# A layer of gated experts on one core: ScalarE in written order in the first unit, result blocks turned back over two units, early operands stored a step later

## The chip, the core and the metric

The kernel runs on one core of one Trainium2 chip. The metric is device microseconds of one execution. Engines are named as in the profile: PE is TensorE, ACT ScalarE, DVE VectorE, POOL GpSimd, and SP is the engine that issues most DMAs.

## What is computed

x has 8 batch rows of 512 x 256 numbers, in float32. Each of 8 experts, and one shared expert, is a gated pair of products and a product back; the results are weighted per batch row and added to x:

```python
g = jnp.einsum('bsd,edf->ebsf', h, Wg)
u = jnp.einsum('bsd,edf->ebsf', h, Wu)
expert_outs = jnp.einsum('ebsf,efd->ebsd', jax.nn.silu(g) * u, Wd)
expert_output = jnp.einsum('be,ebsd->bsd', gating_probs, expert_outs)
shared = jnp.einsum('bsf,fd->bsd', jax.nn.silu(h @ Sg) * (h @ Su), Sd)
sg = shared_gate_prob[:, :, None]
return x + (1.0 - sg) * expert_output + sg * shared
```

D is 256, F is 1024, and no expert is skipped.

## The kernel before

**Units.** The work is cut into 36 units: two halves of the batch (four rows each, `NI` = 4), nine experts, two groups of 512 columns of F. A unit's name is half_expert_group, as in `1_0_1`; `u.n` counts them.

**gate_up (L499).** For each unit the gate and up products of four rows with four blocks of columns are made from fewer matmuls than the plain way needs. Four plain steps give the products of a row with the block of its own number: `P_step` (L335, weight times x) and `Q_step` (L367, into the same bank, with a prepared weight `at` and the other half of x). ScalarE copies P out (L342), DVE makes Q (L375). The twelve products of unlike numbers come in six pairs (`PAIRS`, L59). A pair needs one matmul with differences (`R1_step`, L378: weight difference `u`, operand difference `v`) and two with sums (`R_step`, L389: `wb` and `b`), seeded with sums `z` of P and Q (L354 on POOL, L356 on DVE). `finish` (L320) applies silu on ScalarE (L323) and, on DVE, the product with the up part and the coefficient (L329).

The weights are prepared beside this: `load_w` (L247) issues two loads of 128 KB on SP, `make_at` (L270) makes `at`, `w_difference` (L284) and `w_sums` (L290) make `u` and `wb` on POOL, with prescales on ScalarE (L267). The operands `v` and `b` are made once in each half, in its first unit or ahead of it, are stored in DRAM (`xs`), and are loaded again by each later unit (L190, L207).

**down (L414).** The products back, for the unit before, are 14 groups of two matmuls, so 28 steps, in seven-product form (sums `T` on POOL, L411). Each group takes one of two banks, `po0` and `po1`, in turn (`new_po`, L120). If the bank has not just been used for a transpose (`turned`), ScalarE seeds it with the accumulator (L429) and copies it out at the end (L453); otherwise DVE adds the accumulator (L449). A written string `ORDER` (L561) interleaves the steps of `gate_up` (G) with those of `down` (D); the first unit has `FIRST`.

**Change of half.** In the last unit of the first half, `turn_x` (L141) transposes the four x rows of the second half on PE, and `make_forms` (L164) makes and stores the first three pairs' operands ahead. When the last `down` of that half has completed a block of the result, it is put on the list `ends`. `turn_back` (L478) transposes such a block on PE into the bank last used, ScalarE copies it to `to` (L490; one buffer), POOL adds it to the loaded part of x, `xr` (L491), and SP stores the sum (L494) and loads the next `xr` (two buffers, shared with `xin`). There are eight blocks. A block is taken from the list ahead of a D step (L612), whenever there is one.

**Who sets the order.** PE and POOL run in the written order (`manual_schedule`, L566). ScalarE, DVE and SP are ordered by the scheduler of the language, which may move an instruction ahead of others that it does not depend on. Each DMA has one of eight semaphores in turn, and waits until the DMA before it on the same semaphore has landed. `make_coef` (L96) loads the gates on ScalarE's queue, makes `rest` (L106) and `coef` (L108, L109) on DVE.

Of the kernel before, what the change touches and what calls it, by code (L numbers as in the profile page):

```python
# [9 lines left out]
F32 = mybir.dt.float32  # L10
# [6 lines left out]
def kernel(  # L17
# [31 lines left out]
    nc = tc.nc  # L49
    B, S, D = x.shape  # L50
    E, _, F = Wg.shape
    P = 128
# [6 lines left out]
    PAIRS = ((1, 0), (0, 2), (3, 0), (1, 2), (3, 1), (3, 2))  # L59
    ZBANK = 2  # L60
    LATE = (4, 5)

    const = ctx.enter_context(tc.tile_pool(name="const", bufs=1))
    wpool = ctx.enter_context(tc.tile_pool(name="w", bufs=5))
# [45 lines left out]

    scratch = {}
    back = {}
    xhub = {}


# [48 lines left out]
    def make_forms(h, p):  # L164

        i, j = PAIRS[p]
        d = CI[i] - CI[j]
        v, b0, b1 = (
            zpool.tile([P, S], F32, tag="z", name=f"f{k}{h}_{p}") for k in range(3)
        )  # L170
        ve.tensor_sub(v, xhub[h, i][:, 0], xhub[h, j][:, 0])
        if d != 1.0:
            nc.scalar.mul(v, v, 1.0 / d)
        ve.tensor_add(b0, v, xhub[h, j][:, 1])
        gp.tensor_tensor(b1, v, xhub[h, i][:, 1], ALU.add)
        scratch[h, p] = dram.tile([P, 3, S], F32, tag=f"xs{h}_{p}", name=f"xs{h}_{p}")
        for k, t in enumerate((v, b0, b1)):
            nc.sync.dma_start(scratch[h, p][:, k], t)

    def x_difference(u, p):  # L180

        i, j = PAIRS[p]
        v = vpool.tile([P, S], F32, tag="v", name=f"v{u.name}_{p}")
        if (u.h, p) not in scratch:
            d = CI[i] - CI[j]
            ve.tensor_sub(v, xhub[u.h, i][:, 0], xhub[u.h, j][:, 0])  # L186
            if d != 1.0:
                nc.scalar.mul(v, v, 1.0 / d)
        else:
            nc.sync.dma_start(v, scratch[u.h, p][:, 0])  # L190
        u.V[p] = v

    def x_sums(u, p):


        i, j = PAIRS[p]
        v = u.V[p]
# [72 lines left out]
    def make_at(u, i):  # L270
# [10 lines left out]
        scaled_sum(t, CI[i], raw[:, :, 0], raw[:, :, 1], False)  # L281
        u.at[i] = t

    def w_difference(u, p):  # L284
        i, j = PAIRS[p]
        U = upool.tile([P, 2, P], F32, tag="u", name=f"u{u.name}_{p}")
        gp.tensor_tensor(U, u.at[i], u.at[j], ALU.subtract)  # L287
        u.U[p] = U

    def w_sums(u, p):  # L290
        i, j = PAIRS[p]
        d = CI[i] - CI[j]
        W = bpool.tile([P, 2, 2, P], F32, tag="wb", name=f"wb{u.name}_{p}")
# [41 lines left out]
    def P_step(u, i, m):  # L335
        bank = new_bank(u, m, f"c{i}{i}")
        u.bank[i, i, m] = bank
        nc.tensor.matmul(  # L338
            bank, u.raw[i][:, m, 0], xhub[u.h, i][:, 0], start=True, stop=True
        )  # L340
        t = ppool.tile([P, S], F32, tag="p", name=f"P{i}{m}_{u.name}")
        nc.scalar.copy(t, bank)  # L342
        u.Ps[i, m] = t
        for p in range(ZBANK):
            a, b = PAIRS[p]
            if max(a, b) == i:
                new_z(u, p, m, i, bank if u.n or p else None)

    def new_z(u, p, m, i, bank=None):
# [7 lines left out]
        u.z[i, o, m] = z  # L357

    def make_z(u, p, m):
        if p in LATE:  # L360
            return
        for i in PAIRS[p]:
            o = sum(PAIRS[p]) - i
            if (i, o, m) not in u.z:
                new_z(u, p, m, i)

    def Q_step(u, i, m):  # L367
# [7 lines left out]
        ve.tensor_sub(t, bank, u.Ps[i, m])  # L375
        u.Qs[i, m] = t

    def R1_step(u, p, m):  # L378
        i, j = PAIRS[p]
        bank = new_bank(u, m, f"c{j}{i}")  # L380
# [4 lines left out]
        first = u.Ps if p in LATE else u.z  # L385
        ve.tensor_sub(seed, first[(i, m) if p in LATE else (i, j, m)], bank)  # L386
        ve.tensor_add(bank, bank, first[(j, m) if p in LATE else (j, i, m)])  # L387

    def R_step(u, p, m, r):  # L389
        i, j = PAIRS[p] if r == 0 else PAIRS[p][::-1]  # L390
        bank = u.bank[i, j, m]
        nc.tensor.matmul(  # L392
            bank, u.W[p][:, r, m], u.VB[p][:, r],
            start=False, stop=True, skip_group_check=True,
        )
        if p in LATE:
            ve.tensor_add(bank, bank, u.Qs[j, m])  # L397
        finish(u, m, i, j, bank)

# [99 lines left out]
    def gate_up(u, nxt):  # L499
# [6 lines left out]
            x_sums(u, p)  # L506
            w_sums(u, p)

        for p, make in ((0, w_difference), (0, w_sums), (1, w_difference), (1, w_sums), (2, w_difference)):
            make(u, p)  # L510
        ahead = ((0, x_difference), (0, x_sums), (1, x_difference), (1, x_sums), (2, x_difference))
        if u.n:
            for p, make in ahead:
# [19 lines left out]
        for p in range(len(PAIRS)):  # L533
# [29 lines left out]


    ends = []
    with tc.manual_schedule(engines={mybir.EngineType.PE, mybir.EngineType.Pool}):  # L566
        touch_banks()
        loaded = []
        for i in range(NI):
            loaded.append(load_rows(tpool, "t", i))  # L570
            load_w(units[0], i)
        turning = turn_x(0, tpool, "t", loaded)
        for _ in range(2):
            next(turning)
        for m in range(2):
            P_step(units[0], 0, m)
        for i in range(NI):
            make_at(units[0], i)
        make_coef()
        behind, acc = iter(()), {}  # L580
        for u in units:
            final = u.closes
            nxt = units[u.n + 1] if u.n + 1 < len(units) else None
            g = gate_up(u, nxt)
            nG = 0
            for what in ORDER if u.n else FIRST:
                if what == "G":
                    if nG == 4 and u.n:
                        for _ in behind:
                            pass  # L590
                        pv = units[u.n - 1]
                        load_d(pv, (1,))
                        if pv.opens:
                            acc = {}
                        behind = down(pv, acc, pv.closes)
                        if pv.closes:
                            load_back(pv.h, *BACK[0])
                    if final and nxt is not None:
                        if nG == 18:
                            turning = turn_x(u.h + 1, iopool, "io")  # L600
                        if nG >= 18 and nG % 3 == 0:
                            next(turning, None)
                        if nG in (42, 45, 48):
                            make_forms(u.h + 1, nG // 3 - 14)
                    next(g)
                    nG += 1
                    if nxt is None and nG in (18, 24, 30, 36, 42):
                        next(behind, None)
                elif u.n == 0:
                    for _ in range(2):  # L610
                        next(turning, None)
                else:  # L612
                    if ends:
                        turn_back(*ends.pop(0))
                    next(behind, None)
            for _ in g:
                pass
            for _ in turning:
                pass
        for _ in behind:  # L620
            pass
        pv = units[-1]
        load_d(pv, (1,))
        step, due = 0, []
        for n, at in enumerate(BACK):
            load_back(NH - 1, *at, *((zpool, "z") if n < 6 else (iopool, "io")))
        for _ in down(pv, acc, True):
            step += 1
            if due and due[0] < step:
                due.pop(0)  # L630
                turn_back(*ends.pop(0))
            due += [step + 1] * (len(ends) - len(due))
        for end in ends:
            turn_back(*end)
# [1 line left out]
_INS = [  # L636
    "x",
# [33 lines left out]
```

## Time and profile before

| | |
|---|---|
| median of three runs | 2524.63 us (2524.19 to 2526.6) |
| the profiled execution | 2525.02 us |
| its span, first to last instruction | 2523.2 us |
| mean granted clock of TensorE | 0.998 |
| PE busy | 2499.9 us (99%) |
| POOL busy | 1927.0 us (76%) |
| DVE busy | 1495.5 us (59%) |
| ACT busy | 1143.4 us (45%) |
| matmuls of `gate_up` with sums, L392 | 1728, 594 ns each |
| z on POOL, L354 | 434, 1273 ns each |
| bytes moved | 242.94 MB, 96 GB/s |

A row of the profile's timeline has the start and the length of a run of like instructions, the engine, the line, the operation with its tiles and shape, the number of instructions, and in brackets the time for which the engine was idle before, with what ended it. A busy PE is not one at its peak: the matmuls overlap, so that 594 ns is the length of one, while a row of four starts 1.72 us after the row before it. "PEq", "ACTq" and "SPq" are the sequencers of those engines; a DMA issue stands under them.

### The profile page before, as it was taken

How to read it: one execution, taken by the hardware profiler on the slowest of the kernel's cores; microseconds unless marked ns; L12 is line 12 of the kernel's file. 1: busy time of each engine (PE TensorE's matmuls, PEld its weight loads, DVE VectorE, ACT ScalarE, POOL GpSimd, SP SyncE). 2: the span in 40 equal slices, each digit the busy share in tenths (PEclk: the TensorE clock that was granted, in tenths of full speed). 3: DMA queues.
4: the chain of work that ended last, by engine and by line, in shares of the span. 5: the costliest groups of instructions: out<-in, count | busy, mean ns of one | idle time of the engine just before them, and what ended most of it. 6: DMA issues, size and time to landing. Idle time of an engine off the chain costs nothing.

```text
span 2523.2 us, 22099 instructions
## 1 busy us (share of the span) xinstructions
PE 2499.9 (99%) x5896; PEld 1108.5 (44%) x5896; DVE 1495.5 (59%) x2257; ACT 1143.4 (45%) x2079; POOL 1927.0 (76%) x2073
## 2 busy tenths in 40 slices
PE   8999999999999999999999999999999999999999
PEld 3444444444444444444444444444444444444444
DVE  7655565565555555555775555555565555555556
ACT  3344444444444444444323444444444444444443
POOL 7878877777787777877788777877777777777874
PEclk9999999999999999999999999999999999999999
DMA  5222233233333332233443322232233332332222
GB/s 183 89 86 90 86 94 92 84 101 96 100 92 92 95 90 82 88 96 96 142 140 111 92 89 87 88 95 89 84 101 96 100 93 91 98 89 80 89 84 83
DMA packets 181036, 242.94 MB, mean 96 GB/s; under 512 B 13872, under 2 KB 122416, under 8 KB 180912
## 3 DMA queue, kind: packets, MB, share of 16 engines
q1 hardware_dynamic: 180624, 241.49, 31.5%
q8 instruction: 49, 0.80, 0.1%
q14 instruction: 75, 0.61, 0.1%
q10 hardware_dynamic: 288, 0.04, 0.0%
HBM read 227.84 MB, written 13.63 MB: 96 GB/s over the span
## 4 chain that ended last, share of the span: by engine, by line
PE 95%; POOL 2%; DVE 1%; issue 1%; DMA 0%; ACT 0%; ACTq 0%; SPq 0%; POOLq 0%; DVEq 0%
PE po L438 33%; PE c L392 28%; PE c L382 14%; PE c L338 10%; PE c L369 10%; POOL z L354 1%; POOL T L411 1%; DMA w<-in_L_cond_Wu_dram 0%; POOL wb L268 0%; DMA sgt<-ondB_sharedgateprob_dram 0%; PE pto L129 0%; POOL b L201 0%; POOL u L287 0%; PE ptx L129 0%; DVE v L186 0%
## 5 line engine op out<-in xcount | busy, mean ns | idle before, releaser
L392 PE MATMUL c<-b,wb 128*128 128x512 f32 x1728 | 817.4, 594 | 3.4 <-POOL wb L268 3.4
L354 POOL TENSOR_TENSOR z<-P,Q 128x512 f32<-128x512 f32 x434 | 542.4, 1273 | 110.1 <-DVE Q L375 66.9
L329 DVE SCALAR_TENSOR_TENSOR h<-sg,coef,c 128x512 f32<-128x512 f32 x576 | 427.1, 742 | 239.5 <-PE c L392 230.1
L453 ACT COPY acc<-po 128x512 f32<-128x512 f32 x476 | 278.8, 586 | 584.9 <-PE po L438 582.0
L392 PEld LDWEIGHTS c<-b,wb 128*128 128x128 f32 x1728 | 328.6, 191 | 415.5 <-issue 391.2
L323 ACT ACTIVATE sg<-c 128x512 f32<-128x512 f32 x576 | 342.5, 596 | 367.1 <-PE c L392 202.8
L411 POOL TENSOR_TENSOR T<-h,h 128x512 f32<-128x512 f32 x284 | 358.3, 1277 | 112.1 <-PE po L438 70.4
L438 PE MATMUL po<-T,sd 128*128 128x512 f32 x864 | 435.3, 593 | 2.6 <-ACT po L429 2.6
L382 PE MATMUL c<-v,u 128*128 128x512 f32 x864 | 436.3, 593 | 0.7 <-DVE Q L375 0.7
L386 DVE TENSOR_TENSOR c<-z,c 128x512 f32<-128x512 f32 x288 | 200.1, 695 | 328.0 <-ACT sg L323 256.1
L411 POOL TENSOR_TENSOR T<-h,T 128x512 f32<-128x512 f32 x284 | 356.5, 1276 | 6.7 <-PE po L438 6.7
L268 POOL TENSOR_TENSOR wb<-wb,u 128x256 f32<-128x256 f32 x216 | 154.5, 735 | 206.7 <-ACT wb L267 206.7
L397 DVE TENSOR_TENSOR c<-c,Q 128x512 f32<-128x512 f32 x288 | 200.2, 697 | 188.0 <-PE c L392 188.0
L438 PE MATMUL po<-h,wd 128*128 128x512 f32 x576 | 294.6, 594 | 4.4 <-ACT to L490 4.4
L429 ACT COPY po<-acc 128x512 f32<-128x512 f32 x464 | 273.7, 590 | 36.2 <-DVE acc L455 14.3
L338 PE MATMUL c<-x,w 128*128 128x512 f32 x576 | 276.5, 593 | 2.8 <-ACT sg L323 1.4
L375 DVE TENSOR_TENSOR Q<-c,P 128x512 f32<-128x512 f32 x288 | 198.0, 688 | 106.9 <-ACT sg L323 106.6
L382 PEld LDWEIGHTS c<-v,u 128*128 128x128 f32 x864 | 164.4, 190 | 208.3 <-issue 189.4
L438 PEld LDWEIGHTS po<-T,sd 128*128 128x128 f32 x864 | 163.7, 190 | 208.5 <-issue 188.5
L342 ACT COPY P<-c 128x512 f32<-128x512 f32 x288 | 168.3, 585 | 129.9 <-PE c L338 129.9
L369 PE MATMUL c<-x,at 128*128 128x512 f32 x432 | 203.1, 592 | 1.5 <-DVE z L356 1.5
L387 DVE TENSOR_TENSOR c<-c,z 128x512 f32<-128x512 f32 x288 | 199.5, 693 | 0.9 <-POOL z L354 0.9
(68 smaller groups left out, 1870.8 us busy)
## 6 DMA issues: line engine op xcount, KB each, us to landing
b<-xs SPq DMA_DIRECT2D x207, 512.0 KB, 3.5
v<-xs SPq DMA_DIRECT2D x207, 256.0 KB, 2.6
w<-in_L_cond_Wg_dram SPq DMA_DIRECT2D x128, 128.0 KB, 3.4
w<-in_L_cond_Wu_dram SPq DMA_DIRECT2D x128, 128.0 KB, 3.3
wd<-in_L_cond_Wd_dram SPq DMA_DIRECT2D x64, 256.0 KB, 2.7
xs<-b SPq DMA_DIRECT2D x9, 512.0 KB, 3.1
xin<-in_x_dram SPq DMA_DIRECT2D x16, 256.0 KB, 4.1
xr<-in_x_dram SPq DMA_DIRECT2D x16, 256.0 KB, 3.2
```

Source lines behind the costliest of these rows:

```text
L323: nc.scalar.activation(s, bank, AF.Silu)
L329: ve.scalar_tensor_tensor(t, u.sg[i, j], coef[:, u.e, b : b + 1], bank, ALU.mult, ALU.mult)
L338: nc.tensor.matmul(bank, u.raw[i][:, m, 0], xhub[u.h, i][:, 0], start=True, stop=True)
L354: gp.tensor_tensor(z, u.Ps[i, m], u.Qs[o, m], ALU.add)
L369: nc.tensor.matmul(bank, u.at[i][:, m], xhub[u.h, i][:, 1], start=False, stop=True, skip_group_check=True,)
L382: nc.tensor.matmul(bank, u.U[p][:, m], u.V[p], start=True, stop=True)
L392: nc.tensor.matmul(bank, u.W[p][:, r, m], u.VB[p][:, r], start=False, stop=True, skip_group_check=True,)
L397: ve.tensor_add(bank, bank, u.Qs[j, m])
L411: eng.tensor_tensor(t, a, b, ALU.subtract)
L429: nc.scalar.copy(po, acc[J, x])
L438: nc.tensor.matmul(po, u.wd[I][x], b, start=first, stop=True, skip_group_check=not first,)
L453: nc.scalar.copy(acc[J, x], po)
```

## The change

1. **The first unit.** ScalarE joins PE and POOL in the written order until the first unit's steps are written, and then leaves it: the block of `manual_schedule` is closed and another opened with PE and POOL alone.
2. **The fourth `at`.** `make_at(nxt, 3)`, which was the last one made ahead, is made by the next unit itself, before its third difference.
3. **Stores of the early operands.** `make_forms` no longer stores; it puts the tiles on a list, and `store_made` stores them three G steps later, or before the last pair.
4. **Turnings.** A block of the result is turned only when `since_close`, the number of D steps since the last `down` of the half began, has reached the next of 7, 12, 17, ... 42. Before, a block was turned at the first D step after its completion.
5. **Plain products.** A way of making a pair of the first unit with plain matmuls comes in (`plain`, `plain_step`), and constants `LATE0` and `PLAIN` for it; `PLAIN` is empty and `LATE0` equals `LATE`.

```diff
+    LATE0 = (4, 5)
+    PLAIN = ()
...
         gp.tensor_tensor(b1, v, xhub[h, i][:, 1], ALU.add)
-        scratch[h, p] = dram.tile([P, 3, S], F32, tag=f"xs{h}_{p}", name=f"xs{h}_{p}")
-        for k, t in enumerate((v, b0, b1)):
-            nc.sync.dma_start(scratch[h, p][:, k], t)
+        made.append((h, p, (v, b0, b1)))
+
+    def store_made():
+        for h, p, tiles in made:
+            scratch[h, p] = dram.tile([P, 3, S], F32, tag=f"xs{h}_{p}", name=f"xs{h}_{p}")
+            for k, t in enumerate(tiles):
+                nc.sync.dma_start(scratch[h, p][:, k], t)
+        made.clear()
...
-        for p, make in ((0, w_difference), (0, w_sums), (1, w_difference), (1, w_sums), (2, w_difference)):
+        for p, make in ((0, w_difference), (0, w_sums), (1, w_difference), (1, w_sums)):
             make(u, p)
+        if u.n:
+            make_at(u, 3)
+        w_difference(u, 2)
...
                 if p >= 2:
                     load_w(nxt, p - 2)
-                    make_at(nxt, p - 2)
+                    if p < 5:
+                        make_at(nxt, p - 2)
             store_forms(u)
+            if u.n == 0 and p == 4:
+                for q in PLAIN:
+                    make_forms(0, q)
+            if p == 5:
+                store_made()
...
-    with tc.manual_schedule(engines={mybir.EngineType.PE, mybir.EngineType.Pool}):
+    since_close = 0
+    BACK_AT = [7 + 5 * k for k in range(8)]
+    HAND = {mybir.EngineType.PE, mybir.EngineType.Pool}
+    by_hand = ExitStack()
+    by_hand.enter_context(
+        tc.manual_schedule(engines=HAND | {mybir.EngineType.Activation})
+    )
...
                     if pv.closes:
                         load_back(pv.h, *BACK[0])
+                        since_close = 0
...
                     if nG in (42, 45, 48):
                         make_forms(u.h + 1, nG // 3 - 14)
+                    if nG in (45, 48, 51):
+                        store_made()
...
             else:
-                if ends:
+                since_close += 1
+                if ends and since_close >= BACK_AT[0]:
+                    BACK_AT.pop(0)
                     turn_back(*ends.pop(0))
                 next(behind, None)
         for _ in g:
             pass
+        if u.n == 0:
+            by_hand.close()
+            by_hand.enter_context(tc.manual_schedule(engines=HAND))
```

More of the change, by code (lines that the diff above doesn't have):

```diff
@@ L112 @@
     back = {}
+    made = []
     xhub = {}
@@ L175, in make_forms @@
         gp.tensor_tensor(b1, v, xhub[h, i][:, 1], ALU.add)
[L176 to L178 removed]
+        made.append((h, p, (v, b0, b1)))
[5 more added lines that the diff above has]
+        made.clear()
     def x_difference(u, p):
         i, j = PAIRS[p]
+        if plain(u, p):
+            return
         v = vpool.tile([P, S], F32, tag="v", name=f"v{u.name}_{p}")
@@ L196, in x_sums @@
         i, j = PAIRS[p]
+        if plain(u, p):
+            return
         v = u.V[p]
@@ L282, in make_at, with late, plain @@
         u.at[i] = t
+    def late(u):
+        return LATE if u.n else LATE0
+    def plain(u, p):
+        return u.n == 0 and p in PLAIN
     def w_difference(u, p):
         i, j = PAIRS[p]
+        if plain(u, p):
+            return
         U = upool.tile([P, 2, P], F32, tag="u", name=f"u{u.name}_{p}")
@@ L292, in w_sums @@
         d = CI[i] - CI[j]
+        if plain(u, p):
+            u.W[p] = []
+            for r, (k, c) in enumerate(((i, CI[j]), (j, CI[i]))):
+                a, A = u.raw[k][:, :, 0], u.raw[k][:, :, 1]
+                if c != 0.0:
+                    t = upool.tile([P, 2, P], F32, tag="u", name=f"m{u.name}_{p}_{r}")
+                    scaled_sum(t, c, a, A, False)
+                    A = t
+                u.W[p].append(A)
+            return
         W = bpool.tile([P, 2, 2, P], F32, tag="wb", name=f"wb{u.name}_{p}")
@@ L345, in P_step @@
             a, b = PAIRS[p]
-            if max(a, b) == i:
+            if max(a, b) == i and not plain(u, p):
                 new_z(u, p, m, i, bank if u.n or p else None)
@@ L359, in make_z @@
     def make_z(u, p, m):
-        if p in LATE:
+        if p in late(u) or plain(u, p):
             return
@@ L376, in Q_step, with plain_step @@
         u.Qs[i, m] = t
+    def plain_step(u, p, m, r, k):
+        i, j = PAIRS[p] if r == 0 else PAIRS[p][::-1]
+        if k == 0:
+            u.bank[i, j, m] = new_bank(u, m, f"c{i}{j}")
+        nc.tensor.matmul(
+            u.bank[i, j, m], u.W[p][r][:, m] if k else u.raw[i][:, m, 0],
+            xhub[u.h, j][:, k], start=k == 0, stop=k == 1,
+        )
+        if k:
+            finish(u, m, i, j, u.bank[i, j, m])
     def R1_step(u, p, m):
         i, j = PAIRS[p]
+        if plain(u, p):
+            for k in range(2):
+                plain_step(u, p, m, 0, k)
+            return
         bank = new_bank(u, m, f"c{j}{i}")
@@ L384, in R1_step @@
         u.bank[i, j, m] = seed
-        first = u.Ps if p in LATE else u.z
-        ve.tensor_sub(seed, first[(i, m) if p in LATE else (i, j, m)], bank)
-        ve.tensor_add(bank, bank, first[(j, m) if p in LATE else (j, i, m)])
+        first = u.Ps if p in late(u) else u.z
+        ve.tensor_sub(seed, first[(i, m) if p in late(u) else (i, j, m)], bank)
+        ve.tensor_add(bank, bank, first[(j, m) if p in late(u) else (j, i, m)])
     def R_step(u, p, m, r):
+        if plain(u, p):
+            plain_step(u, p, m, 1, r)
+            return
         i, j = PAIRS[p] if r == 0 else PAIRS[p][::-1]
@@ L395, in R_step @@
         )
-        if p in LATE:
+        if p in late(u):
             ve.tensor_add(bank, bank, u.Qs[j, m])
@@ L565 @@
     ends = []
-    with tc.manual_schedule(engines={mybir.EngineType.PE, mybir.EngineType.Pool}):
[L567 to L610, printed above, removed]
-                        next(turning, None)
-                else:
-                    if ends:
-                        turn_back(*ends.pop(0))
-                    next(behind, None)
[L616 to L620, printed above, removed]
-            pass
[L622 to L634, printed above, removed]
@@ new lines @@
+    since_close = 0
[4 more added lines that the diff above has]
+        tc.manual_schedule(engines=HAND | {mybir.EngineType.Activation})
+    )
+    touch_banks()
+    loaded = []
+    for i in range(NI):
+        loaded.append(load_rows(tpool, "t", i))
+        load_w(units[0], i)
+    turning = turn_x(0, tpool, "t", loaded)
+    for _ in range(2):
+        next(turning)
+    for m in range(2):
+        P_step(units[0], 0, m)
@@ new lines @@
+    for i in range(NI):
+        make_at(units[0], i)
+    make_coef()
+    behind, acc = iter(()), {}
+    for u in units:
+        final = u.closes
+        nxt = units[u.n + 1] if u.n + 1 < len(units) else None
+        g = gate_up(u, nxt)
+        nG = 0
+        for what in ORDER if u.n else FIRST:
+            if what == "G":
+                if nG == 4 and u.n:
+                    for _ in behind:
+                        pass
+                    pv = units[u.n - 1]
+                    load_d(pv, (1,))
+                    if pv.opens:
+                        acc = {}
+                    behind = down(pv, acc, pv.closes)
+                    if pv.closes:
+                        load_back(pv.h, *BACK[0])
+                        since_close = 0
+                if final and nxt is not None:
+                    if nG == 18:
+                        turning = turn_x(u.h + 1, iopool, "io")
+                    if nG >= 18 and nG % 3 == 0:
+                        next(turning, None)
+                    if nG in (42, 45, 48):
+                        make_forms(u.h + 1, nG // 3 - 14)
+                    if nG in (45, 48, 51):
+                        store_made()
+                next(g)
+                nG += 1
+                if nxt is None and nG in (18, 24, 30, 36, 42):
+                    next(behind, None)
+            elif u.n == 0:
+                for _ in range(2):
+                    next(turning, None)
+            else:
+                since_close += 1
+                if ends and since_close >= BACK_AT[0]:
+                    BACK_AT.pop(0)
+                    turn_back(*ends.pop(0))
+                next(behind, None)
+        for _ in g:
+            pass
+        if u.n == 0:
+            by_hand.close()
+            by_hand.enter_context(tc.manual_schedule(engines=HAND))
+        for _ in turning:
+            pass
@@ L636 @@
+    for _ in behind:
+        pass
+    pv = units[-1]
+    load_d(pv, (1,))
+    step, due = 0, []
+    for n, at in enumerate(BACK):
+        load_back(NH - 1, *at, *((zpool, "z") if n < 6 else (iopool, "io")))
+    for _ in down(pv, acc, True):
+        step += 1
+        if due and due[0] < step:
+            due.pop(0)
+            turn_back(*ends.pop(0))
+        due += [step + 1] * (len(ends) - len(due))
+    for end in ends:
+        turn_back(*end)
+    by_hand.close()
 _INS = [
```

## The prediction

> **What bounds the kernel now.** I read the chain of work that ended last first, then TensorE's waits, then the timelines of the stretches where those waits lie.
>
> The chain, section 4 of the page:
>
> ```profile
> PE 95%; POOL 2%; DVE 1%; issue 1%; DMA 0%; ACT 0%; ACTq 0%; SPq 0%; POOLq 0%; DVEq 0%
> ```
>
> TensorE is the bound: only its stalls can be won, and a delay elsewhere costs only where TensorE then waits. Its waits by line (total us, times, longest), those over 0.4 us:
>
> ```profile
> PE po L438 <- ACT to L490: 4.4, 2, 3.6
> PE c L392 <- POOL wb L268: 3.4, 1, 3.4
> PE po L438 <- ACT po L429: 2.6, 2, 2.2
> PE c L369 <- DVE z L356: 1.5, 1, 1.5
> PE c L338 <- ACT sg L323: 1.4, 1, 1.4
> ...
> PE c L338 <- DVE h L329: 0.5, 1, 0.5
> ```
>
> Nearly every wait happens once or twice in 36 units, so the middle is gap-free (rows of four matmuls repeat every 1.72 us). I added up each matmul's start-to-start excess over 0.429 us (0.109 for a transpose): 29.1 us in all, 13.6 in the first unit (before 70 us), about 13 around the change of half (1192 to 1340), 1.8 at the end. So 26.6 us are within reach. Three parts of the change reach there.
>
> Part of the excess is a slowed clock after a stall. The stretches right behind three stalls (columns: time, busy and count of PE, PEld, DVE, ACT, POOL, then granted clock, DMA share, GB/s):
>
> ```profile
> 50.30:53.60 3.30, 3.30 (x5) 1.24 (x5) 1.30 (x2) 1.05 (x2) 3.30 (x5) 0.50 0.26 86
> ...
> 1238.10:1241.50 3.40, 3.40 (x5) 1.35 (x4) 1.77 (x3) 1.58 (x4) 3.32 (x6) 0.50 0.96 323
> ...
> 1289.30:1292.70 3.40, 3.32 (x4) 1.52 (x5) 0.00 (x0) 0.03 (x1) 3.39 (x4) 0.50 0.64 234
> ```
>
> Clock 0.50 for 3.41 us, so about 1.7 us lost each, on top of the stall.
>
> [...]
>
> **Turnings spread (the largest part).** Eight result blocks are turned at the start of the second half. Before, a turn-back comes at `down` steps 8, 12, 14, 16, 22, 26, 28 and the first step of the next `down`. Its chain is TensorE transpose, ScalarE copy into `to` (L490, one buffer), GpSimd add (L491, the only reader that frees `to`), store. TensorE, GpSimd and ScalarE at the cluster:
>
> ```profile
> 1283.38 0.66 PE L129 MATMUL pto<-ident,acc 128*128 128x128 f32 x4 [0.69 <-DVE acc L459]
> ...
> 1289.38 1.22 PE L438 MATMUL po<-h,wd 128*128 128x512 f32 x1 [3.62 <-ACT to L490]
> ```
> ```profile
> 1287.45 1.26 POOL L491 TENSOR_TENSOR xr<-to,xr 128x512 f32<-128x512 f32 x1
> ```
> ```profile
> 1288.74 0.59 ACT L490 COPY to<-pto 128x512 f32<-128x512 f32 x1 [5.42 <-POOL xr L491]
> ```
>
> GpSimd reaches the first block's add only at 1287.45, as 4.8 us of z, b and wb work stand ahead in its written order; the second copy waits for it; TensorE waits 3.6 us because the bank it wants is being turned. Gone with a distance of five steps: that stall (3.79 by starts), the 0.86 at 1283.38 (the accumulator is then long ready) and the slow window (1.74). The eighth turning's 1.00 at 1330.25 (0.73 of wait) also goes from its place. Sum 7.4.
>
> New: five steps is odd, and a bank alternates with each step. The after order puts turnings at steps 8, 12, 17, 22, 27, 32, 37, 42. At an odd step the bank just turned is the one that the very next `po` matmul needs, as at the eighth turning before:
>
> ```profile
> 1330.25 1.12 PE L438 MATMUL po<-h,wd 128*128 128x512 f32 x2 [0.73 <-ACT to L490]
> ```
>
> Three odd steps (17, 27, 37) at 0.9 to 1.0 each: +2.8. It would be 0 only if other matmuls stood between the transposes and `po`; the order shows none, but ScalarE could be quicker, so 0 is the lower end. It would be 3.8 each if the ScalarE copy again waited for a late add; a unit has 28 steps in 69 us, so five steps are about 12 us, and the add was done 6.1 us after the backlog began (4.8 + 1.26): excluded.
>
> Turning earlier triggers something else. A `w` load of the next unit stands on SP behind a store and a reload of result blocks; I place its landing at 1304.9 to 1305.4 (1306.03 before), while TensorE arrives some 5.5 us earlier at the P matmul that waits, over a ScalarE copy queued behind that landing. Slack before was 3.2 us: a stall of 0 to 2.3 us. I take 0.6, nearer to 0 as the load moves too. GpSimd's added waits for `to` in the next unit (z 3.4 to 4.6 us later) lie under slacks of 5 to 8 us: 0. If that cover failed, the excess would come one to one.
> Net: −7.4 +2.8 +0.6 = **−4.0** (−7.4, if nothing comes in their place, to −7.4 +3.0 +2.3 = −2.1).
>
> **ScalarE in written order, first unit.** The two coefficient DMAs are issued first of all on ScalarE today (0.73 and 1.17); `rest` is the first DVE op to use them:
>
> ```profile
> 1.17 0.46 ACTq L104 DMA_DIRECT2D sgt<-ondB_sharedgateprob_dram  x1
> ```
> ```profile
> 6.68 0.17 DVE L106 TENSOR_SCALAR rest<-sgt 128x8 f32<-128x8 f32 x1 [5.55 <-DMA sgt<-ondB_sharedgateprob_dram]
> ```
>
> In written order both issues stand behind the second P copy (10.28 before) and, by the built order, each waits for a `w` load's landing on its semaphore (12.14 and 13.64 before). Behind them in ScalarE's queue stands the copy of x1 (10.76 before), which becomes about 13.3. On DVE `rest` moves behind Q00, and all later DVE work is behind it. The issue at about 13.3 lands, call it at T, 2.6 us later at best (the page's median for the reloads of v), 5.5 as this DMA took before (some 0.5 of spread in the issue added), so T = 15.8 to 19.3. I take 17.3, between the two: SP's loads issued at 11 to 13 took 5 to 6 us, but this one is 4 KB and on a queue of its own.
>
> [...] The same transfer took 5.5 us in this trace.
>
> What that costs: between `rest` and x2 stand `coef` (0.17 and 0.71), v (0.81), h, Q01, x2 itself (0.7 each): x2 ends at T+3.4 (15.36 before). From x2 to Q10, the same nine ops, DVE took 6.9 us (15.36 to 22.30); where GpSimd stands still beside them the b and v ops (1.06 to 1.21) may go as fast as the others (0.7), some 1.0 less. So Q10 ends at T+9.3 to T+10.3. TensorE runs late by up to 5 us, but it has 3.4 us to wait for GpSimd's wb (the L392 row above) and 1.5 and 0.7 us to wait for DVE, so its delay vanishes. GpSimd sets that wait: it works without a gap from 13.58 to 54 us, and the z that needs Q10 started at 24.68: it slips by T − 15.4 to T − 14.4, which is 0.4 to 4.9, and 2.4 in the middle at T = 17.3, one to one into the 3.4 us stall. What I credit: GpSimd starts 0.3 earlier (second `w` loads issued at 3.6 instead of 5.07; the rate of landings allows 0 to 0.5), and at the boundary of units the Q step is put ahead of P, which fills the 0.6 us wait for h (by starts 0.7). ScalarE no longer copying x0 behind the coefficients (0.55) helps only TensorE's slack: 0. The 1.4 us wait of L338 stays, since the ScalarE at-copy that waits for its load still stands ahead of the activation.
> Net: +2.4 −0.3 −0.7 = **+1.4** (−0.8 at T = 15.8 and the earliest start, +4.2 at T = 19.3 and no earlier start).
>
> **The fourth `at` made a unit later.** A GpSimd op of 0.73 us moves past a block of GpSimd's written order in each of 35 units. There GpSimd waited anyway (1.72 us at the first, 3.22 at the change of half), TensorE for nothing: 0. If it were on the path it would be 0.7 per unit, up to 25 us; 76% busy GpSimd speaks against it.
>
> **Stores of early operands a step later.** In the built order SP's sequence around them is the same instruction by instruction, so the `w` load behind a store of forms, and with it the stall of 2.19 (2.35 by starts) before the matmul of 1236.87 and its slow window, stay: 0. If the reordering had taken effect it would be up to −4.1. The new constants for plain products are empty or unchanged; that code adds nothing.
>
> **Sum.** −4.0 + 1.4 = −2.6 from the profiled execution's 2525.02 (span 2523.2 and 1.8 around it): 2522.4. That execution stands 0.4 above the median of the runs, 2524.63; by the median it is 2522.0. About 0.2% (5.05 us) is what a measurement of this kernel can tell from no change.
>
> **Rivals.**
> 1. *Coefficients late, and slower than before* (17%). The whole of DVE's first-unit work, and GpSimd's z behind it, slip one to one with T. It turns the sign when T − 14.9 − 1.0 exceeds what the turnings give: from T = 19.9 at 4.0, from 18.0 at 2.1. With T of 20 to 23 the loss is 4.1 to 7.1, and with 2.1 to 4.0 given back the time is 2525 to 2529.5. For it: SP's `wd` loads issued at 11.5 took 6.1 us, and an issue that waits for two landings is late when either is. Against: TensorE's spare time of 5.6 us, and the size.
> 2. *All of the gain* (20%). T below 16, odd turnings hidden, no new stall: −7.4 −0.8 from the median: 2516.4, or 2517.4 with one odd turning in view. For it: the 12 us distance. Against: the 0.73 row.
> 3. *The `w` load eats it* (15%). 2.3 us at the P matmul of the next unit and a slow window of 1.7 after it: −2.6 −0.6 +2.3 +1.7 = +0.8, about 2525.4. For it: the 2.19 us wait that had its window.
> 4. *The stores move after all*: the built order excludes it.
> The likeliest (48%): 2519.7 to 2524.3, almost all of it within 0.2%. Faster by over 0.2% (below 2519.6): the second and little of the likeliest, 22%. Slower by over 0.2% (above 2529.7): the first rival reaches it only with T past 23 or a slow window on top, which I give 7 of its 17%, and 2 points of the third: 9%. Within: 69%. Range: 2517, so that most of the second case is in, to 2528, which takes in the bounds of the costs (−8.2 to +2.1) and all but the far part of the first: 1 in 10 below, 1 in 10 above.
>
> **What would show it.** In the profile after: no wait on L490 above 1 us but three of 0.7 (three rows of L438 <- ACT to); no 0.50 window near 1289; `rest` between 15.8 and 19.3; the L392 <- POOL wb wait about as long as TensorE's lateness leaves, its end at 48.9 + 2.1; the 2.2 us L429 wait still there; the L338 <- DVE h wait gone. Wrong if `rest` lies past 20, if L338 <- ACT sg grows past 2 us near 1300, or if GpSimd's `at` shows up as a releaser in the middle.

## The result and the profile after

| | median, us | runs |
|---|---|---|
| before | 2524.98 | 8 (2524.19 to 2526.6) |
| changed | 2531.86 | 8 (2530.04 to 2532.87) |

The ratio is 1.0024, 95% interval [1.0014, 1.0033]: slower by 6.9 us, and outside the range of the forecast (2517 to 2528). The profiled execution of the changed kernel took 2530.74 us, with a span of 2528.3.

First the chain, then TensorE's waits of the changed kernel (engine, line waited for: total us, times, longest), to be laid beside those of before. Lines have moved: L338 is now L370, L392 is L442, L438 is L488, L490 is L540, L429 is L479.

```profile
PE 96%; DVE 1%; POOL 1%; DMA 1%; issue 1%; ACT 0%; SPq 0%; ACTq 0%; DVEq 0%; POOLq 0%
```

```profile
PE ptx L133 <- DVE x L159: 5.7, 1, 5.7
PE c L370 <- ACT sg L355: 3.7, 2, 2.6
PE po L488 <- ACT po L479: 3.0, 3, 2.4
PE po L488 <- ACT to L540: 2.3, 3, 0.8
...
PE c L429 <- DVE h L361: 1.8, 1, 1.8
...
PE c L442 <- POOL wb L281: 0.4, 1, 0.4
```

The 3.6 us wait of a `po` matmul for `to` has gone, and three short ones stand there, as forecast. The wait for `wb` has shrunk from 3.4 to 0.4, not because `wb` is earlier, but because TensorE is late: it now waits 5.7 us for an x tile of the first unit. Where one P matmul waited for sg, 1.4 us at the end of the first unit, two do: that one, now 2.6, and one of 1.2 at 1313.

By stretches of TensorE's own rows (the start of the same matmul in both profiles): the `po` matmul that follows the last x tile of the second half comes at 1227.3 instead of 1220.7, 6.6 us late. From there to a `po` matmul in the last `down` the changed kernel wins 1.9 us back (2500.9 against 2496.2). The last 27 us differ by 0.4. So the first unit loses 6.6 us where 1.4 was forecast, and the turnings bring 1.9 where 4.0 was.

The first unit's loss in VectorE's timeline of the changed kernel, behind the landing of the coefficients:

```profile
17.54 0.67 DVE L109 TENSOR_SCALAR rest<-sgt 128x8 f32<-128x8 f32 x1 [3.06 <-DMA sgt<-ondB_sharedgateprob_dram]
...
18.20 1.76 DVE L197 TENSOR_TENSOR v<-x,x 128x512 f32<-128x512 f32 x1
19.88 0.69 DVE L111 TENSOR_TENSOR coef<-gt,rest 128x8 f32<-128x8 f32 x8
...
21.75 0.67 DVE L159 SCALAR_TENSOR_TENSOR x<-x,ptx 128x512 f32<-128x512 f32 x1
...
27.89 0.68 DVE L197 TENSOR_TENSOR v<-x,x 128x512 f32<-128x512 f32 x1
```

GpSimd in the same stretch, and below it the z that needs Q10 in the kernel before:

```profile
18.14 1.26 POOL L386 TENSOR_TENSOR z<-P,Q 128x512 f32<-128x512 f32 x1
21.97 1.27 POOL L386 TENSOR_TENSOR z<-P,Q 128x512 f32<-128x512 f32 x1 [2.57 <-DVE Q L407]
...
29.25 2.60 POOL L386 TENSOR_TENSOR z<-P,Q 128x512 f32<-128x512 f32 x2 [4.35 <-DVE Q L407]
```

```profile
24.68 2.50 POOL L354 TENSOR_TENSOR z<-P,Q 128x512 f32<-128x512 f32 x2
```

The landing is at 17.5, as forecast. But the operand difference `v` takes 1.76 us beside a running z of GpSimd, and 0.68 where GpSimd stands still; `rest` takes 0.67 instead of 0.17. GpSimd's z that needs Q10 starts at 29.25 instead of 24.68. VectorE works without a gap from the landing to Q10. Behind TensorE's wait of 5.7 us the granted clock is 0.50 until 26.1; that is no term of its own, since TensorE waits for `wb` later on.

The second half of the loss is at the end of the first unit. TensorE and ScalarE there before:

```profile
58.73 1.88 PE L392 MATMUL c<-b,wb 128*128 128x512 f32 x4
62.04 1.13 PE L338 MATMUL c<-x,w 128*128 128x512 f32 x2 [1.43 <-ACT sg L323]
```

```profile
60.60 0.42 ACT L267 ACTIVATE at<-w 128x256 f32<-128x256 f32 x1 [4.32 <-DMA w<-in_L_cond_Wu_dram]
60.92 1.07 ACT L323 ACTIVATE sg<-c 128x512 f32<-128x512 f32 x2
```

And in the changed kernel:

```profile
62.83 1.88 PE L442 MATMUL c<-b,wb 128*128 128x512 f32 x4
67.31 2.07 PE L370 MATMUL c<-x,w 128*128 128x512 f32 x2 [2.60 <-ACT sg L355]
69.17 2.54 PE L442 MATMUL c<-b,wb 128*128 128x512 f32 x4
```

```profile
65.86 0.42 ACT L280 ACTIVATE at<-w 128x256 f32<-128x256 f32 x1 [5.49 <-DMA w<-in_L_cond_Wu_dram]
66.19 1.06 ACT L355 ACTIVATE sg<-c 128x512 f32<-128x512 f32 x2
```

ScalarE stands for 5.49 us at the prescale of the fourth `at`, which waits for a weight load; behind it are the two silus that free the bank for TensorE's P matmul. So it was before, too, but the load landed 5.3 us earlier. Behind the stall the granted clock is half:

```profile
67.10:70.40 3.30, 3.09 (x4) 1.51 (x5) 3.30 (x6) 0.74 (x2) 3.22 (x7) 0.50 0.72 269
```

### The profile page after: what moved, and what is told of

Its sections match the earlier page's. It is cut to its first block, busy times and chain, and to the rows that moved or that the text cites. A ratio compares the mean times of both kernels' runs of the same rounds, so it can differ in the third digit from the quotient of the medians.

```text
span 2528.3 us, 22097 instructions
## 1 busy us (share of the span) xinstructions
PE 2501.1 (99%) x5896; PEld 1109.2 (44%) x5896; DVE 1494.2 (59%) x2256; ACT 1143.1 (45%) x2081; POOL 1924.8 (76%) x2073
## 4 chain that ended last, share of the span: by engine, by line
PE 96%; DVE 1%; POOL 1%; DMA 1%; issue 1%; ACT 0%; SPq 0%; ACTq 0%; DVEq 0%; POOLq 0%
PE po L488 34%; PE c L442 29%; PE c L429 14%; PE c L401 10%; PE c L370 9%; DMA w<-in_L_cond_Wu_dram 0%; POOL z L386 0%; PE pto L133 0%; POOL T L461 0%; DMA sgt<-ondB_sharedgateprob_dram 0%; PE ptx L133 0%; DMA xin<-in_x_dram 0%; DMA w<-in_L_cond_Wg_dram 0%; DVE h L361 0%; POOL wb L281 0%
## 5 line engine op out<-in xcount | busy, mean ns | idle before, releaser
L442 PE MATMUL c<-b,wb 128*128 128x512 f32 x1728 | 816.4, 594 | 0.4 <-POOL wb L281 0.4
L442 PEld LDWEIGHTS c<-b,wb 128*128 128x128 f32 x1728 | 328.4, 190 | 411.7 <-issue 391.0
L488 PE MATMUL po<-T,sd 128*128 128x512 f32 x864 | 435.5, 593 | 4.6 <-ACT po L479 3.0
L429 PE MATMUL c<-v,u 128*128 128x512 f32 x864 | 435.6, 592 | 2.5 <-DVE h L361 1.8
L488 PE MATMUL po<-h,wd 128*128 128x512 f32 x576 | 293.5, 592 | 0.0
L479 ACT COPY po<-acc 128x512 f32<-128x512 f32 x465 | 274.4, 590 | 38.8 <-DVE acc L505 19.3
L370 PE MATMUL c<-x,w 128*128 128x512 f32 x576 | 278.9, 597 | 4.1 <-ACT sg L355 3.7
L429 PEld LDWEIGHTS c<-v,u 128*128 128x128 f32 x864 | 163.9, 190 | 210.0 <-issue 189.5
L488 PEld LDWEIGHTS po<-T,sd 128*128 128x128 f32 x864 | 163.4, 190 | 210.4 <-issue 186.8
```

The source lines that it names most:

```text
L370: nc.tensor.matmul(bank, u.raw[i][:, m, 0], xhub[u.h, i][:, 0], start=True, stop=True)
L442: nc.tensor.matmul(bank, u.W[p][:, r, m], u.VB[p][:, r], start=False, stop=True, skip_group_check=True,)
L479: nc.scalar.copy(po, acc[J, x])
L488: nc.tensor.matmul(po, u.wd[I][x], b, start=first, stop=True, skip_group_check=not first,)
```

## The experiments

Each run is compared with runs of the kernel before on the same chip, whose median is given with it. A ratio has its 95% interval. The theory after the result was that the first unit's 6.6 us are all due to the late coefficients.

### ScalarE back to the scheduler

```diff
-        tc.manual_schedule(engines=HAND | {mybir.EngineType.Activation})
+        tc.manual_schedule(engines=HAND)
```

> The changed kernel with ScalarE left to the scheduler in the first unit, all else as changed. Theory (the first unit loses 6.6 us because the coefficients' DMAs are issued late in ScalarE's written order, so that DVE's and then GpSimd's work slips) and its first rival (the written order of ScalarE's other work is at fault) both expect the first unit back at the time of before: 2525.0 less the 1.9 us that the turnings save = 2523.1 us, rest at about 6.7 us, no half-clock window before 45 us. Second rival (the fourth at, made a unit later, is at fault): 2529 us or more.

Measured: 2523.66 against 2525.62, ratio 0.9991 [0.9982, 1.0]. `rest` is at 6.66, and the time is that of the turnings' saving alone: the loss comes with ScalarE's written order. It does not say by which of its parts. One expectation missed: there is a half-clock stretch at 8.5 us. The kernel before, in runs whose first part is unchanged, has one there at times as well (at 7.4 with only the turnings, at 7.7 with only the fourth `at`; none ahead of 50.2 in its own profile). So a single profile's first unit is uncertain by some 1.4 us, an estimate from the run with only the turnings, where the `po` matmul behind the last x tile comes at 1222.1 instead of 1220.7.

### Only ScalarE in written order

To the kernel before, only the two `manual_schedule` blocks are added.

> The kernel before, with ScalarE in written order in the first unit and nothing else. Theory and first rival: 2525.0 + 6.6 = 2531.6 us, with the matmul at line 338 that waited for sg 1.4 us before now waiting about 2.6. Second rival (the fourth at): 2525 us.

Measured: 2528.24 against 2525.62, ratio 1.0009 [1.0, 1.0018]. 2.6 us instead of 6.6: **the theory fell**. TensorE reaches the end of the first unit as late as in the changed kernel, but the first P matmul then goes on at once:

```profile
62.87 1.88 PE L392 MATMUL c<-b,wb 128*128 128x512 f32 x4
64.63 1.13 PE L338 MATMUL c<-x,w 128*128 128x512 f32 x2
```

The order on ScalarE says why. In this kernel the fourth `at` is still made in the first unit, thus in written order, and its prescale stands behind the two silus (at 66.56, and they at 63.38). In the changed kernel it is made by the next unit, outside the written stretch, and the scheduler puts it ahead of them.

### The coefficients first

The changed kernel, with the two DMAs written ahead of everything; the arithmetic on them stays where it was.

```diff
+    load_coef()
     touch_banks()
```

> The changed kernel, ScalarE still in written order, but the two coefficient DMAs written first of all, so that they are issued at about 0.7 and 1.2 us; the arithmetic on them is written where it was. Theory: the first unit is back at the time of before or 0.7 better (the Q step that stands ahead of P), so 2522.4 to 2523.1 us, rest at about 7 us. First rival (ScalarE's written order itself): 2530 to 2532 us.

Measured: 2524.77 against 2525.62, ratio 0.9995 [0.9986, 1.0004], 1.7 us above the theory's bound and 5 below the rival's. The coefficients are out of the way, and the stall at the P matmul is there, 3.34 us by starts, with its half clock. Both parts exist, then.

### Only the turnings

> The kernel before with the turnings at steps 7, 12, 17 and so on, and nothing else. Theory (the turnings save 7.4, and give back three stalls of 1.0 at odd steps and 2.2 at the matmul that waits for a weight load): 2525.0 - 1.9 = 2523.1 us. Rival (part of the saving came from another part of the change): 2524.5 to 2525 us.

Measured: 2524.23 against 2525.62, ratio 0.9993 [0.9985, 1.0002], 1.4 us less, which the interval does not set apart from none. In the profile the stretch from the `po` matmul behind the last x tile (1220.7 before, 1222.1 here) to TensorE's last transposes is 2.2 us shorter than before, with the three odd waits of 1.0.

### Coefficients first, fourth `at` where it was

The kernel before, ScalarE in written order in the first unit, the DMAs first. The new theory names two causes: late coefficients, and the fourth `at` outside the written stretch.

> The kernel before, with ScalarE in written order in the first unit and the coefficient DMAs written first; the fourth at is made where it was. New theory (of the 6.6 us, about half is the late coefficients, and the rest comes from the fourth at: made by the next unit it lies outside the written stretch, and its ScalarE prescale, which waits for a weight load, goes ahead of two silus that the next matmul waits for): the 1.6 us stall of before at the first P matmul of the second unit is gone, and with it nothing comes: 2525.5 - 1.6 - 0.7 = about 2523 us. Rival (only the coefficients matter, and the two halves are one): 2525 us, with the stall still there.

Measured: 2523.3 against 2525.52, ratio 0.999 [0.9981, 0.9998]. As forecast, and the stall has gone: written order in the first unit gains, if the coefficients are early and the prescale is in it.

### The changed kernel with the fourth `at` where it was

```diff
-                    if p < 5:
-                        make_at(nxt, p - 2)
+                    make_at(nxt, p - 2)
```

(and the call in the next unit taken out)

> The changed kernel with the fourth at made by the unit before, as it was; the coefficients stay late. New theory: the stall of 2.76 us and the half-clock window of 1.7 at the end of the first unit go, the matmul at 64 us goes on at once: 2531.9 - 4 = about 2527.5 us. Rival (the stall is a consequence of the late coefficients alone): 2531 to 2532 us.

Measured: 2526.58 against 2525.52, ratio 1.0004 [0.9996, 1.0013]. Against the changed kernel's 6.9 above before, this is 1.1 above: by the medians the moved `at` costs 5.8 us of the changed kernel. By TensorE's rows it is 3.2: from the last four sums of the first unit to the row of eight P matmuls in the second, TensorE takes 9.8 us here, 13.0 in the changed kernel and 11.1 before. (The profiled run of the changed kernel lies 1.1 us below its median, that of this one 0.9 above.) ScalarE and TensorE at the end of the first unit:

```profile
63.49 1.19 ACT L355 ACTIVATE sg<-c 128x512 f32<-128x512 f32 x2 [2.95 <-DVE c L447]
66.27 0.42 ACT L280 ACTIVATE at<-w 128x256 f32<-128x256 f32 x1 [1.58 <-DMA w<-in_L_cond_Wu_dram]
```

```profile
62.99 1.88 PE L442 MATMUL c<-b,wb 128*128 128x512 f32 x4
64.74 1.13 PE L370 MATMUL c<-x,w 128*128 128x512 f32 x2
```

The same load lands as late, but the silus are in front of it, and TensorE goes on.

### Turnings at even steps

```diff
+    BACK_AT = [8, 12, 18, 22, 28, 32, 38, 42]
```

> The kernel before with the turnings at the even steps 8, 12, 18, 22, 28, 32, 38, 42, and nothing else. Theory (a turning at an odd step stalls the next matmul into the same bank for 1.0 us): the three stalls of 1.0 are gone, 2524.2 - 3.0 = about 2521.2 us. Rival (the stall moves to the next wait, that of the P matmul for sg near 1306 us, which grows by as much): 2523 to 2524 us.

Measured: 2521.42 against 2525.52, ratio 0.9983 [0.9974, 0.9992]. The three waits for `to` are gone. The wait near 1306 did grow, from 1.1 in the run with only the turnings to 2.2 by starts, less than the rival had it:

```profile
1306.60 1.12 PE L338 MATMUL c<-x,w 128*128 128x512 f32 x2 [2.00 <-ACT sg L323]
```

### Only the fourth `at`

> The kernel before with the fourth at made by the next unit, and nothing else; ScalarE is left to the scheduler. New theory: the scheduler had the prescale ahead of the two silus already, so nothing changes on ScalarE: 2525.5 us, stall of about 1.6 at the first P matmul of the second unit. Rival (the moved op itself costs time): above 2527 us.

Measured: 2526.67 against 2525.52, ratio 1.0005 [0.9996, 1.0014]. No measurable cost while the scheduler orders ScalarE anyway. The median lies between theory and rival, and the first unit's half-clock stretches in its profile (two, at 7.7 and 24.8) are as large as the difference. The stall was not 1.6 us as expected but 3.1. Yet the P matmul behind it comes at 63.74, and at 63.49 in the run with only the turnings, whose first unit is as before and whose profile also has an early half-clock stretch, at 7.4. Beside that run the moved `at` shows as 0.3 us at this place.

### Only the later stores

> The kernel before with the stores of the early operands a step later, and nothing else. Theory (SP's order does not change): 2525.5 us, the stall of 2.3 us near 1235 us as before. Rival (the later store lets a weight load go ahead): the stall gone, 2521.5 us.

Measured: 2525.89 against 2525.93, ratio 1.0001 [0.9993, 1.001]. Nothing, as forecast.

### The best parts together

> The kernel before with ScalarE in written order in the first unit, the coefficient DMAs first, the fourth at where it was, and the turnings at even steps. Theory (the two gains lie in different stretches and add up): 2523.3 - 4.1 = about 2519.2 us. Rival (the clock windows or the loads take one of them back): 2521 to 2523 us.

Measured: 2518.95 against 2525.93, ratio 0.9971 [0.996, 0.9983]. The two gains add up.

### ScalarE in written order throughout

```diff
-            by_hand.enter_context(tc.manual_schedule(engines=HAND))
+            by_hand.enter_context(tc.manual_schedule(engines=HAND | {mybir.EngineType.Activation}))
```

> As the run with the best parts, but with ScalarE in written order in all units. Theory (the stall of 2.3 us near 1235 us and that of about 2 near 1305 have the same cause as that at the end of the first unit, a prescale that waits for a load ahead of work that TensorE needs; written order puts it behind): 2519.2 - 4 = about 2515 us, or more than 2525 us if another op in written order waits in each unit. Rival (in the steady units the scheduler's order is needed): above 2530 us.

Measured: 3013.98 against 2525.93, ratio 1.1932 [1.1916, 1.1948]. The rival holds. TensorE's waits there:

```profile
PE po L445 <- ACT po L436: 312.6, 386, 3.1
PE po L445 <- POOL wb L275: 44.9, 31, 1.4
```

In each unit the copy that seeds a `po` bank stands behind prescales or silus that wait for work of TensorE or VectorE not yet done. The scheduler's order keeps it ahead.

### The fourth `at` without ScalarE

As the best parts, with the `at` of units 18 and 19 made by GpSimd alone, in two additions, as in the first unit.

```diff
-        if u.n == 0 and CI[i] == 2.0:
+        if u.n in (0, 18, 19) and CI[i] == 2.0:
```

> As the run with the best parts, but the fourth at of units 18 and 19 is made on GpSimd alone, in two additions, as that of the first unit is, so that ScalarE has no prescale there that waits for a weight load. Theory (the stalls of 2.4 us near 1232 and 2.5 near 1301 are ScalarE's, blocked by that prescale with work behind it that TensorE needs): both stalls and the half-clock window after the first go, 2518.95 - 2.4 - 1.7 - 2.5 = about 2512.5 us. Rival (the load itself is what TensorE waits for, or GpSimd's one more addition of 0.73 us in each takes its place): 2517 to 2519 us.

Measured: 2512.03 against 2525.7, ratio 0.9949 [0.9937, 0.9961]; five of six runs lie between 2511.5 and 2512.7, one at 2520.15. This is the fastest version, 0.8% below the changed kernel by the medians. Both stalls are gone, and the stretches where they were have TensorE busy at full clock:

```profile
1229.00:1238.00 9.00, 9.00 (x23) 3.97 (x22) 6.80 (x11) 4.72 (x10) 6.10 (x7) 1.00 0.67 203
1296.00:1304.00 8.00, 8.00 (x23) 3.81 (x22) 7.90 (x14) 3.56 (x6) 7.92 (x8) 1.00 0.84 275
```

### The coefficients one turning later

The kernel before, ScalarE in written order in the first unit, and `make_coef` behind the copy of x1. (One D less at the start of `FIRST`, whose two turnings are written ahead of it.)

> The kernel before, ScalarE in written order in the first unit, and the coefficients loaded one turning later, behind the copy of x1 on ScalarE; the fourth at where it was. In the built order VectorE has the first difference and sum ahead of rest, and the third x tile right behind it. Theory (the landing stays near 17 us, and the excess came from the operand difference of 1.75 us and the sum that ran beside GpSimd between the landing and the third x tile): the third x tile is ready about 1.5 us after the landing instead of 4.9, Q10 2 us earlier than with the coefficients after the second P copy, and the time 2528.2 - 2 = about 2526 us. Rival (all of the cost is in the landing): 2528 us or more.

Measured: 2526.03 against 2526.3, ratio 0.9999 [0.999, 1.0008]. The landing was later, at 19.1, 1.6 later than with the coefficients behind the second P copy, and the kernel still 2.9 us better against before (−0.3 instead of +2.6). VectorE:

```profile
19.14 0.80 DVE L106 TENSOR_SCALAR rest<-sgt 128x8 f32<-128x8 f32 x1 [4.84 <-DMA sgt<-ondB_sharedgateprob_dram]
...
19.93 0.67 DVE L155 SCALAR_TENSOR_TENSOR x<-x,ptx 128x512 f32<-128x512 f32 x1
```

The third x tile is ready at 20.6, 1.5 us after the landing, and Q10 at 27.8 instead of 29.2. So a later landing cost less. In this order x1 is copied ahead of the two DMAs, and VectorE makes `v` and `b` while it waits for them: by this run the work left behind the landing counts for more than the landing.

### The coefficients one step earlier

> The kernel before, ScalarE in written order in the first unit, and the coefficient DMAs written behind the copy of x0, ahead of the first P copy; the fourth at where it was. They wait for the landings of an x and a w load (9 and 10 us), so the coefficients land near 15.5 us, and rest stands ahead of x1 on VectorE. Theory (the first unit slips with the landing and with what VectorE has behind it): Q10 ends near 27 us, against 22.3 before and 29.2 with the coefficients after the second P copy, and the time is 2525 to 2526.5 us. Rival (the first unit is bound elsewhere, and only a landing past 17 us costs): 2523.3 us, as with the coefficients first.

Measured: 2527.82 against 2526.3, ratio 1.001 [1.0001, 1.0019]. The landing was at 15.3, and yet Q10 ended at 28.9, not near 27, and the time is above what the theory had. One row explains most of it:

```profile
16.00 2.31 DVE L115 TENSOR_TENSOR coef<-gt,rest 128x8 f32<-128x8 f32 x8
```

Eight small products that took 0.69 take 2.31 us; in the kernel before GpSimd makes `u` and `wb` at that time (14.26 to 19.20). The slope "one to one with T", T being the landing, is thus wrong both ways: 1.6 later was better, 2.2 earlier gained 0.2 in Q10.

## Why the prediction was wrong

**The fourth `at` at nothing: the step that failed.** The text said: "A GpSimd op of 0.73 us moves past a block of GpSimd's written order in each of 35 units." For GpSimd that held, as the run with only the fourth `at` shows. But `make_at` issues two instructions, and the other is ScalarE's prescale. Moved into the next unit, it left the stretch that the same change puts in written order. The text even looked at this place, and had the 1.4 us wait stay "since the ScalarE at-copy that waits for its load still stands ahead of the activation". That was true of the built order, but where ScalarE is in written order it is true only because the `at` was moved: with the `at` kept, the prescale comes behind the silus, and the stall is gone. With it moved, the stall grew with the later landing and a half-clock stretch followed it. At this boundary 0.7 us was to be won; 2.0 were lost, and with the `at` kept 1.2 are won. Keeping the `at` takes 5.8 us off the changed kernel by the medians, 3.2 by TensorE's rows; the two parts of the change, each harmless or even good in the right company, work against each other.

**The late coefficients: right mechanism, wrong size.** The landing was forecast at 17.3 and came at 17.5, by luck: the issue was at 12.2 and not at 13.3, and the load took 5.3 us and not 4.0. GpSimd's z was forecast to slip by 2.4 and slipped 4.6. Of the missing 2.2, 1.5 lies between landing and x2: 4.9 us where 3.4 was summed, because `v` was priced at 0.81 and took 1.76, `rest` at 0.17 and took 0.67. The text had allowed for the neighbour only as a gain ("some 1.0 less"). (From x2 to Q10 it counted nine ops; the rows have eight, in the same 6.9 us.) Behind z, GpSimd waited twice more (0.42 and 0.95), and `wb` came 6.1 us late, where the sign given was "its end at 48.9 + 2.1". What hid a part: the stall of 3.5 us of before shrank to 0.6, and its slow window went with it. TensorE's last sums of the first unit then came 4.1 us late, against 2.1 in the forecast's sum.

By the time, late coefficients cost 4.8 us with the `at` kept (2.6 above before against 2.2 below it), and 7.7 in the changed kernel, where it is moved (6.9 above against 0.85 below). So neither term alone explains the miss: the `at` was priced at nothing, and the coefficients at half of what they cost.

**The turnings: right, smaller.** The sum was −7.4 + 2.8 + 0.6. Measured in the profiles: the 7.4 are gone, the odd steps gave 3.1, the P matmul's wait for the load 1.4 (bounds were 0 to 2.3, the value taken 0.6), a few short waits behind it 0.8, and the wait near 1241 is 0.2 longer: −1.9.

**The stores, the Q step ahead of P and the odd step's price** came as forecast: 0, no wait for h at the boundary any more, 1.0 to 1.1 where 0.9 to 1.0 was said.

**The rivals.** The slow side was named for the coefficients alone, and to be decided by a landing past 18 to 20 us. The landing was earlier than that, and it became slower all the same. A wait for sg past 2 us was among the signs of being wrong, but near 1300; it came at the end of the first unit.

**The chances.** Slower by over 0.2% had 9%. The median is 0.27% slower.

## What to carry to other kernels

A helper that is moved takes all its instructions along, and each has to be followed on its own engine: here a second one, of 0.42 us, left a written stretch and was put ahead of work that the busiest engine needed. In an engine's queue look for an instruction that waits for a load and ask what stands behind it; making the `at` on an engine that has time ("The fourth `at` without ScalarE") brought 6.9 us, as much as all the reordering together (7.0). And an op's price is that of a row with the same neighbour: a difference of two tiles took 0.68 or 1.76 us, depending on whether GpSimd ran beside it.

## What the runs showed of the hardware

**VectorE beside GpSimd.** VectorE's `v` and `b`, whose operands are two tiles in SBUF, took longer where GpSimd computed. In the changed kernel they took 0.68 us each while it stood still (25.98 and 27.89), and 1.76, 1.44 and 1.75 beside it (18.20, 22.35 and 23.71). In the kernel before, where GpSimd works on from 13.58, they took 1.06 to 1.21 (15.29 to 20.44), while the ops that read a bank of TensorE's (x tile, Q, h) stayed at 0.67 to 0.74 in the same stretch. The `v` of 1.76 us started 0.06 after a z that took 1.26, and ended 0.56 after it, near its own length alone. Why it is so was not shown.

**Half clock beside a wait: the length alone did not decide.** In the profile of the kernel before, the granted clock is 0.50 for 3.41 us from 50.25, 1238.08 and 1289.28, beside waits of TensorE's of 3.35, 2.19 and 3.62 us. In that of the changed kernel it is 0.50 for 6.83 us from 19.30, and for 3.41 us from 67.08 and 1244.68, beside waits of 5.73, 2.60 and 2.42. But a wait of 2.21 us there (11.00 to 13.21) has none: the clock is 1.00 from 5.65 to 19.29. With the coefficients first and the fourth `at` where it was, the wait that was 2.19 us before took 2.20 (1232.96 to 1235.16) and had none; in the run with only the fourth `at` one of 3.10 us (60.64 to 63.74) had none either.

What did decide was not shown; an estimate can be made from the times. In both profiles the starts lie whole multiples of 3.413 us, the length of one stretch, apart: 348 from 50.245 to 1238.083 and 15 from there to 1289.283 before, 14 from 19.295 to 67.082 and 345 from there to 1244.680 after. Marked off at that distance, the wait of 2.19 us (1234.68 to 1236.87) lies between two marks, 1234.67 and 1238.08, while a mark at 12.47 cuts the one of 2.21 us into 1.5 and 0.7. By the slow stretches of their own profiles (one starts at 1285.54, one ends at 28.17) the one of 2.20 us is cut into 1.4 and 0.8, and the one of 3.10 into 1.7 and 1.4. So in these four cases a wait of 2.2 to 3.1 us cost its length, or 1.7 us more, and by the estimate it was its place that made the difference.
